# A four-layer image network on one core: five small moves at the seams between its layers

## The chip, the core and the metric

The kernel runs on one core of a Trainium2 chip. A core has five engines with queues of their own: TensorE (PE in the profile; its weight loads are PEld), VectorE (DVE), ScalarE (ACT), GpSimd (POOL) and SyncE (SP), which here only issues transfers. An engine works through its queue in order, and waits on semaphores for what the others have to finish first. The metric is the time of one execution on the device, in microseconds, as the median of the runs shown.

## The reference

Input is a batch of two images of 512 channels x 64 x 64, in fp32. Four layers are applied one after another, each as x = x + layer(groupnorm(x)):

```python
def _gn(v, G=32, eps=1e-5):
    g = v.reshape(B_, G, C_ // G, H_, W_)
    m = mean(g, (2, 3, 4)); s = var(g, (2, 3, 4))
    return ((g - m) / sqrt(s + eps)).reshape(v.shape)

# layer 0: local attention (3x3 window) joined with attention to 16x16 pooled tokens
q = xf @ W_q + b_q;  kv = xf @ W_kv + b_kv
xs = layernorm(mean of gelu(xf @ W_sr + b_sr) over 4x4) ;  kvp = xs @ W_kv + b_kv
attn = softmax(concat([q_scaled . k_local (9), q_scaled . k_pool (256)]))
out = ((lt @ v_local) + (a_pool @ v_pool)) @ W_proj + b_proj

# layer 1: deformable attention: offsets from the query, bilinear samples as keys and values
q = w_q x;  off = tanh(w_off2 gelu(q[::4, ::4] * w_off1 + b_off1)) * 4
kv = w_kv grid_sample(q, grid + off)
out = w_out (softmax(q k / 8) v) + b_out

# layer 2: max pools of 1, 3, ..., 13, mixed by two weights for each channel
s = relu(w2 relu(w1 mean(x) + b1) + b2);  q_s = clip(floor(s), 0, 5)
out = (s - q_s) * pools[q_s + 1] + (q_s + 1 - s) * pools[q_s] + x

# layer 3: linear attention with 256 random features for each of 8 heads
out = (qp @ (kp^T v)) / (qp . sum(kp)) @ Wo
```

All attention has 8 heads of 64 channels.

## The kernel before

An image is held in SBUF as 4 chunks of 128 channels (KC = 4) by 4096 positions; a second buffer of the same size (Y) takes what a layer makes. Positions are worked in 8 blocks of 512 (NB = 8, TB = 512), which is one PSUM bank. The two images are worked one after the other, and in an image the layers one after the other; the seams between layers are interleaved by hand, with Python generators whose `yield` marks where another step may come in. The order of instructions on an engine is the order in which the program writes them, as a tile scheduler rearranges it; a place where the program wants an instruction behind a certain other one is written as `with tc.issue_after(ins)`. For layer 2's last channel chunk VectorE is set to manual schedule, so the order there is as written.

A tile of PSUM or SBUF comes from a pool with a number of buffers. To write into a buffer that comes round again, the writer waits for the last reader of it. Waits are kept for a whole tile, not for parts of it.

**Layer 0** (class Local) goes through 16 units, 4 for each channel chunk, of 1024 positions each. `weigh(u)` (L2677 and following) multiplies the values by nine weights ("taps"), which SyncE fetches from `rows` (L2677), and adds them up on GpSimd (L2706) into `out`, a tile called late in the profile. At its end the unit's result is stored to `yd` in DRAM (L2712), on SyncE's queue. Three of the four passes of the output projection (`output(c4)`, fetches at L2289) read parts of `yd` back; for c4 of 2 and 3 the last chunk is taken from `self.out` in SBUF instead. So units 14 and 15 are never read back from DRAM; unit 13 is, by output(1). Units 13 and 14 are the ones that the change touches.

**Layer 1** starts with `query_and_sample`: a small projection of thinned-out positions fills the four banks of `acc`, from which ScalarE makes off_t (L1255) and VectorE makes bq (L1009, from products of L1006), and then the queries of block 0 are projected (L134, tile wq). Attention follows: `exponentials`, `attended` (psO), `inverse_sums` and `divided`, in a pipeline over blocks and chunks. `inverse_sums` collects the sums of the softmax of the 8 heads in one bank: chunk cc's two heads are rows 32 cc and 32 cc + 1 (L1520), of 32 rows each. VectorE takes the reciprocal of the whole bank in two halves (L1526); `divided` spreads two rows for each chunk over 128 partitions with a product (L1534) and multiplies by it (L1537). `add_output` (L1227, L1230, L1232) projects, adds to the image and takes statistics.

**The seam from layer 1 to layer 2.** For the last block, the statistics of each chunk are joined (L1116), and `pool_mixture` finds from them the mixture weights: L1187 (means of groups), L1188 to L1191, L1194, and on to L1209. Layer 2's horizontal maxima (`across_rows`, L698) are started here, rows by rows, where VectorE has room: rows 0 to 10 and 55 to 64 last (the 128x620 and 128x558 of the profile).

**Layer 2** (`pool_chunk`) goes through the channel chunks. For each it makes larger and larger max pools on VectorE by `spread_max` (L698 for the middle, ScalarE's L699 for edges), and adds the pool of width 2j + 1, times a weight for each channel, into 8 PSUM banks with diagonal weights (L1403), j from 0 to 6. In the last chunk the eighth bank is lent to the statistics of the next group norm until late: the products of block 7 for j < 5 are kept in a list and given out after the fourth product of j = 5. `stats_in_steps` has two steps: means of groups (L965 to L968), and, behind its `yield`, the product L970, nmean on ScalarE (L971), L972 on VectorE and the power on GpSimd (L973). The steps are called at j = 4 and j = 5. At j = 5 the weights of layer 3 are scaled by the result (L1433).

Of the kernel before, what the change touches and what calls it, by code (L numbers as in the profile page):

```python
# [9 lines left out]
F32 = mybir.dt.float32  # L10
# [6 lines left out]
P = 128  # L17
C = 512
KC = C // P
W = 64  # L20
# [913 lines left out]
class Net(General):  # L934
# [22 lines left out]
        for _ in self.stats_in_steps(ks, pp.tile([P, TB], F32, name="mm") if ps is None else ps):  # L957
            pass

    def stats_in_steps(self, ks, ps):  # L960

        nc, mv = self.nc, self.mv
        nmean, rstd, cent, var = (self.stats[:, i, ks] for i in range(4))
        n = ks.stop - ks.start
        nc.tensor.matmul(ps[:, :n], self.grp, mv[:, ks, 0], start=True, stop=True)  # L965
        nc.vector.tensor_tensor(cent, mv[:, ks, 0], ps[:, :n], ALU.subtract)
        nc.vector.tensor_tensor(var, cent, cent, ALU.mult)
        nc.vector.tensor_tensor(var, var, mv[:, ks, 1], ALU.add)  # L968
        yield
        nc.tensor.matmul(ps[:, KC:KC + n], self.grp, var, start=True, stop=True)  # L970
        nc.scalar.mul(nmean, ps[:, :n], -1.0)  # L971
        nc.vector.tensor_scalar(var, ps[:, KC:KC + n], 1e-5, None, ALU.add)  # L972
        nc.gpsimd.tensor_tensor(rstd, var, self.mhalf[:, :n], ALU.pow)  # L973
# [63 lines left out]
    def layer1(self, X, Y, d):  # L1037
# [6 lines left out]
        with tc.tile_pool(name="l1", bufs=1) as sp:  # L1044
# [13 lines left out]
            with tc.tile_pool(name="l1c", bufs=1) as late:  # L1058
# [17 lines left out]
                with tc.tile_pool(name="l1b", bufs=2) as wp, \  # L1076
                        tc.tile_pool(name="l1s", bufs=6, space=PSUM) as pp, \
                        tc.tile_pool(name="l1o", bufs=2, space=PSUM) as ppo:
                    st = wp.tile([P, KC, NB, 6], F32, name="gn_st1", bufs=1)
                    w1 = wp.tile([P, KC, 32], F32, name="w1", bufs=1)  # L1080
                    nc.sync.dma_start(w1, d["w1"].rearrange("(kc p) e -> p kc e", p=P))
                    w2 = wp.tile([32, C], F32, name="w2", bufs=1)
                    nc.sync.dma_start(w2, d["w2"])
                    wo = wp.tile([P, KC, C], F32, name="wo1", bufs=1)
                    nc.sync.dma_start(wo, d["w_out1"].rearrange("(kc p) o -> p kc o", p=P))
                    steps = [(blk, cc) for blk in range(NB) for cc in range(KC)]
                    part = lambda blk, cc=slice(0, KC): Y[:, cc, blk * TB:(blk + 1) * TB]
                    flat = lambda a: a.rearrange("p k o -> p (k o)")
                    probs, totals, later = {}, {}, []
                    rows3 = self.scratch[:, :KC * 10 * W].rearrange("p (k y x) -> p k y x", k=KC, x=W)  # L1090
                    ring = cycle([a[:, n:n + TB] for a, lo, hi in (
                        (flat(wq), 0, KC), (flat(wkv), 5, 8), (flat(feats), 0, 2),
                        (wp.tile([P, 3 * TB], F32, name="totals", bufs=1), 0, 3))
                        for n in range(lo * TB, hi * TB, TB)]).__next__
                    for i in range(len(steps) + 4 + KC):
                        if i < len(steps):
                            blk, cc = steps[i]
                            probs[i], totals[i] = self.exponentials(part(blk, cc), keys[:, cc, :],
                                                                    ring, wp, pp)
                        if 1 <= i <= len(steps):  # L1100
                            blk, cc = steps[i - 1]
                            self.attended(part(blk, cc), probs.pop(i - 1),
                                          vals[:, :, cc * P:(cc + 1) * P], ppo)
                        at = lambda n: i >= n and (i - n) % KC == KC - 1 and (i - n) // KC
                        if (blk := at(1)) is not False and blk < NB:
                            r = self.inverse_sums([totals.pop(KC * blk + n) for n in range(KC)], wp,
                                                  pp)
                        if (blk := at(2)) is not False and blk < NB:
                            self.divided(part(blk), r, pp)
                        if (blk := at(3)) is not False and blk < NB:  # L1110
                            later += [(blk, oc) for oc in range(KC)]
                        if later:
                            blk, oc = later.pop(0)
                            self.add_output(X, wo, part(blk), blk, oc, st, pp)
                            if blk == NB - 1:
                                nc.vector.bn_aggr(self.mv[:, oc, :],  # L1116
                                                  st[:, oc].rearrange("p b s -> p (b s)"))
                                if oc < 2:
                                    self.maxima_across(X, NB - 2, rows3, slice(oc, oc + 1))
                                    self.maxima_down(Y, NB - 2, rows3, slice(oc, oc + 1))  # L1120
                                for rows in ([(20, 32), (32, 44)], [(10, 20), (44, 55)],
                                             [], [])[oc]:
                                    self.across_rows(Y, slice(*rows))
                            elif oc == KC - 1 and blk < NB - 2:
                                self.maxima_across(X, blk, rows3, slice(0, KC))
                                self.maxima_down(Y, blk, rows3, slice(0, KC))
                    mixture = self.pool_mixture(w1, w2, wp, pp)
                    next(mixture)
                    self.maxima_across(X, NB - 1, rows3, slice(0, 1))
                    self.maxima_down(Y, NB - 1, rows3, slice(0, 1))  # L1130
                    for rows in (0, 10), (55, W):
                        self.across_rows(Y, slice(*rows))
                    next(mixture)

    def maxima_across(self, X, blk, h, ks):
# [145 lines left out]
    def query_and_sample(self, X, Y, wq, bq, grid, feats, top, wp, pp, ppk):  # L1281
# [9 lines left out]

        def query(blk):
            for cc in range(KC):
                ps = pp.tile([P, TB], F32, name="mm")
                self.project(ps, wq[:, :, cc * P:(cc + 1) * P], X, blk)
                nc.scalar.activation(Y[:, cc, blk * TB:(blk + 1) * TB], ps, AF.Identity,
                                     bias=bq[:, cc:cc + 1])
                yield
            nc.vector.tensor_reduce(top[:, :, blk], Y[:, :, blk * TB:(blk + 1) * TB], AX.X, ALU.max,
                                    apply_absolute_value=True)  # L1300
# [85 lines left out]
    def pool_chunk(self, X, Y, cc, c0, d0, wts, sp):  # L1386
# [7 lines left out]
            self.pools.insert(0, Y[:, cc - 1, :])  # L1394
        h = image(self.scratch)
        accs, kept = self.accs, []
        stats = self.stats_in_steps(slice(0, KC - 1), accs[NB - 1])
        if cc == KC - 1:
            self.diags = cycle([next(self.diags), next(self.diags),
                                *[sp.tile([P, P], F32, name=f"diag{i}") for i in range(2, 7)]])  # L1400
# [5 lines left out]
        def add(w, src, j):  # L1406
            dg = next(self.diags)
            nc.scalar.activation(dg, self.ident, AF.Copy, scale=w)  # L1408
            for b in range(NB):
                if b == NB - 1 and cc == KC - 1 and j < 5:  # L1410
                    kept.append((b, dg, src, j))
                else:
                    product(b, dg, src, j)
                while kept and j == 5 and b == 3:
                    product(*kept.pop(0))

        add(c0[:, cc:cc + 1], x2, 0)
        flat = Y[:, cc, :]
        for j in range(1, 7):
            if j > 1:  # L1420
                last, flat = image(flat), self.pools.pop(0)
                self.pools.append(flat)
                if cc or j > 2:
                    self.spread_max(h, last, 2)
                self.spread_max(image(flat), h, 1)
                if cc == KC - 1 and j in (4, 5):
                    next(stats, None)
                if cc == KC - 1 and j == 3:
                    self.moments(sp)
                if cc == KC - 1 and j == 5:  # L1430
                    for w in self.wkv3:
                        for kc in range(KC - 1):
                            nc.scalar.activation(w[:, kc], w[:, kc], AF.Copy,  # L1433
                                                 scale=self.stats[:, 1, kc:kc + 1])
            add(wts[:, j, cc:cc + 1], flat, j)
# [78 lines left out]
    def inverse_sums(self, totals, wp, pp):  # L1514
# [6 lines left out]
                                 self.cst[:, C_EVEN + h:C_EVEN + h + 32], totals[cc][h],  # L1521
                                 start=(h == 0), stop=(h == 1))
        r = wp.tile([P, TB], F32, name="recip")
        for i in range(2):
            half = slice(i * TB // 2, (i + 1) * TB // 2)
            nc.vector.reciprocal(r[:, half], psD[:, half])  # L1526
        return r

    def divided(self, att, r, pp):
# [475 lines left out]
class Local:  # L2005
# [673 lines left out]
    def weigh(self, u):  # L2679
# [29 lines left out]
            if i < 9:  # L2709
                yield  # L2710
        lo = u % self.UN * self.UT
        nc.sync.dma_start(self.yd[:, cc, lo:lo + self.UT], out)  # L2712
        yield


# [187 lines left out]
```

## Time and profile before

| | us |
|---|---|
| median of 3 runs | 4915.69 |
| lowest, highest | 4914.85, 4920.11 |
| the profiled execution | 4912.44 |
| its span in the trace | 4910.6 |
| TensorE busy | 4726.7 (96%) |
| VectorE busy | 2983.6 (61%) |
| ScalarE busy | 1851.7 (38%) |
| GpSimd busy | 1815.6 (37%) |

The mean granted clock of TensorE in the profiled execution is 0.989 of full speed. In a row of a timeline the columns are the start and the duration in us, engine, line and operation, what is written and read, and, in square brackets, how long the engine was idle before it and what it waited for. A matmul of fp32 with 512 columns appears as two records in the trace. Most of the product groups follow one another without a gap: TensorE's idle time in the whole span is 4910.6 - 4726.7 = 183.9 us. As an example of a group of SyncE's transfers, there are 32 stores to yd of 512 KB each, and 432 fetches of 256 KB each from rows.

### The profile page before, as it was taken

How to read it: one execution, taken by the hardware profiler on the slowest of the kernel's cores; microseconds unless marked ns; L12 is line 12 of the kernel's file. 1: busy time of each engine (PE TensorE's matmuls, PEld its weight loads, DVE VectorE, ACT ScalarE, POOL GpSimd, SP SyncE). 2: the span in 40 equal slices, each digit the busy share in tenths (PEclk: the TensorE clock that was granted, in tenths of full speed). 3: DMA queues.
4: the chain of work that ended last, by engine and by line, in shares of the span. 5: the costliest groups of instructions: out<-in, count | busy, mean ns of one | idle time of the engine just before them, and what ended most of it. 6: DMA issues, size and time to landing. Idle time of an engine off the chain costs nothing. (4 is left out here: it accounts for less than half of the span.)

```text
span 4910.6 us, 48474 instructions
## 1 busy us (share of the span) xinstructions
PE 4726.7 (96%) x16883; PEld 1965.5 (40%) x16883; DVE 2983.6 (61%) x4044; ACT 1851.7 (38%) x3555; POOL 1815.6 (37%) x1164
## 2 busy tenths in 40 slices
PE   7999999999999999999999999999999999999999
PEld 3433332555334444433344333325543344444333
DVE  4267777754679633377633677777536795334766
ACT  1256665334323233323212566652443233333222
POOL 0036666501320045545400466665013201454544
PEclk9999999999999999999999999999999999999999
DMA  4035556600000000111120455565000000000111
GB/s 157 1 94 156 154 157 169 178 24 10 1 0 19 1 1 1 56 55 56 65 78 2 108 156 157 156 172 160 20 10 1 2 17 1 1 1 18 44 50 46
DMA packets 129441, 313.30 MB, mean 64 GB/s; under 512 B 23394, under 2 KB 36194, under 8 KB 127652
## 3 DMA queue, kind: packets, MB, share of 16 engines
q1 hardware_dynamic: 129188, 310.12, 21.8%
q8 instruction: 135, 2.21, 0.2%
q14 instruction: 118, 0.97, 0.1%
HBM read 260.73 MB, written 49.31 MB: 63 GB/s over the span
## 5 line engine op out<-in xcount | busy, mean ns | idle before, releaser
L134 PE MATMUL mm<-big,w 128*128 128x512 f32 x2496 | 1157.8, 608 | 19.1 <-DVE big L2485 13.6
L134 PEld LDWEIGHTS mm<-big,w 128*128 128x128 f32 x2496 | 453.1, 191 | 689.7 <-issue 549.0
L2706 POOL TENSOR_TENSOR late<-late,big 128x1024 f32<-128x1024 f32 x194 | 459.2, 2367 | 216.6 <-DVE big L2701 174.4
L1702 POOL TENSOR_TENSOR big<-big 128x512 f32<-128x512 f32 x224 | 277.6, 1271 | 219.3 <-ACT big L1693 219.3
L2526 DVE TENSOR_TENSOR prods<-qs,big 128x2048 f32<-128x2048 f32 (+1 forms) x184 | 330.7, 1819 | 34.3 <-PE tap L2564 23.7
L2701 DVE TENSOR_TENSOR big<-big,mm 128x512 f32<-128x512 f32 x388 | 252.4, 682 | 104.6 <-ACT mm L2693 103.2
L1693 ACT ACTIVATE big<-mm,ed 128x256 f32<-128x256 f32 x512 | 194.1, 490 | 232.7 <-DVE top L1689 200.3
L2693 ACT COPY mm<-big 128x512 f32<-128x512 f32 x432 | 245.4, 597 | 80.3 <-DMA big<-rows 46.1
L2706 POOL TENSOR_TENSOR late<-late,tap 128x1024 f32<-128x1024 f32 x94 | 222.0, 2361 | 97.8 <-DVE tap L2701 83.7
L1501 POOL TENSOR_TENSOR wq<-prob 128x512 f32<-128x512 f32 x48 | 71.9, 1520 | 486.3 <-ACT prob L1498 474.8
L1689 DVE TENSOR_REDUCE top<-mm 128x1 f32<-128x512 f32 x256 | 159.0, 683 | 148.2 <-PE mm L1620 148.2
L2611 POOL TENSOR_TENSOR late<-late 128x512 f32<-128x512 f32 x76 | 95.4, 1275 | 395.7 <-ACT late L2596 379.5
L134 PE MATMUL mm<-big,wq 128*128 128x512 f32 x512 | 235.0, 604 | 2.7 <-ACT off_t L1255 2.7
L1227 PE MATMUL mm<-big,wo 128*128 128x512 f32 x512 | 237.6, 610 | 0.0
L1667 PE MATMUL mm<-w,big 128*128 128x512 f32 x512 | 234.5, 601 | 0.0
L1403 PE MATMUL acc<-big,diag 128*128 128x512 f32 x512 | 227.7, 602 | 5.2 <-ACT diag L1408 4.6
L1961 PE MATMUL mm<-k,w 128*128 128x512 f32 x512 | 232.0, 600 | 0.7 <-DVE big L1964 0.7
L973 POOL TENSOR_TENSOR group_stats<-group_stats,cst 128x1 f32<-128x1 f32 (+1 forms) x20 | 20.2, 1024 | 543.0 <-DVE group_stats L972 489.7
L134 PE MATMUL mm<-big,big 128*128 128x512 f32 x464 | 201.7, 594 | 0.5 <-DVE b_sr L1011 0.5
L1926 POOL TENSOR_SCALAR qf_sum<-qf,ksum_ratio 128x512 f32<-128x512 f32 x64 | 100.4, 1570 | 264.2 <-PE psD L1944 212.4
L1498 ACT ACTIVATE prob<-mm 128x512 f32<-128x512 f32 x256 | 133.3, 602 | 171.3 <-PE mm L1495 171.1
L2564 PE MATMUL tap<-prods,cst 128*32 128x512 f32 x1152 | 183.2, 604 | 11.5 <-DVE prods L2526 7.4
(432 smaller groups left out, 8118.7 us busy)
## 6 DMA issues: line engine op xcount, KB each, us to landing
big<-rows SPq DMA_DIRECT2D x432, 256.0 KB
tap<-rows SPq DMA_DIRECT2D x208, 256.0 KB
yd<-late SPq DMA_DIRECT2D x32, 512.0 KB
lost_all<-lost SPq DMA_DIRECT2D x128, 128.0 KB
out<-big SPq DMA_DIRECT2D x64, 256.0 KB
big<-in_W_kv SPq DMA_DIRECT2D x8, 1024.0 KB
rows<-late SPq DMA_DIRECT2D x64, 128.0 KB
big<-in_x SPq DMA_DIRECT2D x32, 256.0 KB
```

The source lines that it names most:

```text
L134: self.nc.tensor.matmul(ps, w[:, kc, :], X[:, kc, blk * TB:(blk + 1) * TB], start=(kc == 0), stop=(kc == KC - 1))
L1227: nc.tensor.matmul(ps, w[:, kc, oc * P:(oc + 1) * P], att[:, kc, :], start=(kc == 0), stop=(kc == KC - 1))
L1403: nc.tensor.matmul(accs[b], dg, src[:, b * TB:(b + 1) * TB], start=(j == 0), stop=(j == 6))
L1667: nc.tensor.matmul(ps, X[:, kc, lo:lo + P], wv[:, kc, :], start=(kc == 0), stop=(kc == KC - 1))
L1693: nc.scalar.activation(f[:, t, :], pS[h][i][:, t % 2, :], AF.Exp, bias=ed[:, t, 2 * cc + h:2 * cc + h + 1])
L1702: nc.gpsimd.tensor_tensor(a, a, part, ALU.add)
L1961: nc.tensor.matmul(ps, self.wo[:, kc, oc * P:(oc + 1) * P], qs[:, kc, :], start=(kc == 0), stop=(kc == KC - 1))
L2526: self.nc.vector.tensor_tensor(self.pair(u, k)[:, :n].rearrange("p k (y x) -> p k y x", x=W), bcast(qs.rearrange("p (y x) -> p y x", x=W), ...
L2564: nc.tensor.matmul(ps[32 * q:32 * q + 32, :], self.cst[:, C_TAPW + 16 - 2 * k:][:, :32], self.pair(u, k)[:, 0, j * TB:(j + 1) * TB], start ...
L2693: nc.scalar.copy(ps, part)
L2701: nc.vector.tensor_tensor(part.rearrange("p (y x) -> p y x", x=W), self.vx[:, y:y + self.UY // 2, dx:dx + W], ps.rearrange("p (y x) -> p y ...
L2706: nc.gpsimd.tensor_tensor(out, out, t, ALU.add)
```

## The change

Five places are edited.

- A: `inverse_sums` transposes the bank in 32x32 squares, so that the two rows of each 32 that carry sums become two columns, takes the reciprocal of those columns alone (128x32), and transposes back.
- B: the maxima of rows 0 to 10 and 55 to 64 are issued behind the last chunk's aggregate (L1116), where before they could come ahead of it.
- C: in layer 2's last chunk, `stats_in_steps` gets one more `yield`, between L970 and L971; both of its first steps are called at j = 4, and the last one between the two maxima of j = 5. The kept products are given out ahead of j = 5's products, not after its fourth.
- D: the first query of layer 1 takes the last bank of `acc` in place of a bank of the pool.
- E: the stores of units 13 and 14 go on GpSimd's queue.

```diff
-    def stats_in_steps(self, ks, ps):
+    def stats_in_steps(self, ks, ps, split=False):
...
         nc.tensor.matmul(ps[:, KC:KC + n], self.grp, var, start=True, stop=True)
+        if split:
+            yield
         nc.scalar.mul(nmean, ps[:, :n], -1.0)
         nc.vector.tensor_scalar(var, ps[:, KC:KC + n], 1e-5, None, ALU.add)
         nc.gpsimd.tensor_tensor(rstd, var, self.mhalf[:, :n], ALU.pow)
...
                             if blk == NB - 1:
-                                nc.vector.bn_aggr(self.mv[:, oc, :],
-                                                  st[:, oc].rearrange("p b s -> p (b s)"))
+                                mean = nc.vector.bn_aggr(
+                                    self.mv[:, oc, :], st[:, oc].rearrange("p b s -> p (b s)"))
...
-                    for rows in (0, 10), (55, W):
-                        self.across_rows(Y, slice(*rows))
+                    with tc.issue_after(mean.ins):
+                        for rows in (0, 10), (55, W):
+                            self.across_rows(Y, slice(*rows))
                     next(mixture)
...
-                ps = pp.tile([P, TB], F32, name="mm")
+                ps = acc[:, KC - 1] if not blk + cc else pp.tile([P, TB], F32, name="mm")
                 self.project(ps, wq[:, :, cc * P:(cc + 1) * P], X, blk)
...
-        stats = self.stats_in_steps(slice(0, KC - 1), accs[NB - 1])
+        stats = self.stats_in_steps(slice(0, KC - 1), accs[NB - 1], True)
...
             nc.scalar.activation(dg, self.ident, AF.Copy, scale=w)
+            while kept and j == 5:
+                product(*kept.pop(0))
             for b in range(NB):
                 if b == NB - 1 and cc == KC - 1 and j < 5:
                     kept.append((b, dg, src, j))
                 else:
                     product(b, dg, src, j)
-                while kept and j == 5 and b == 3:
-                    product(*kept.pop(0))
...
                     self.spread_max(h, last, 2)
+                if cc == KC - 1 and j == 5:
+                    next(stats, None)
                 self.spread_max(image(flat), h, 1)
-                if cc == KC - 1 and j in (4, 5):
-                    next(stats, None)
+                if cc == KC - 1 and j == 4:
+                    next(stats)
+                    next(stats)
...
         r = wp.tile([P, TB], F32, name="recip")
-        for i in range(2):
-            half = slice(i * TB // 2, (i + 1) * TB // 2)
-            nc.vector.reciprocal(r[:, half], psD[:, half])
+        nc.vector.transpose(psD, psD)
+        two = psD.rearrange("p (b n r) -> p b n r", n=16, r=2)[:, :, 0]
+        nc.vector.reciprocal(two, two)
+        nc.vector.transpose(r.rearrange("p (b n r) -> p b n r", n=16, r=2), bcast(two, 2, 16))
         return r
...
         lo = u % self.UN * self.UT
-        nc.sync.dma_start(self.yd[:, cc, lo:lo + self.UT], out)
+        queue = nc.gpsimd if 2 <= KC * self.UN - u <= 3 else nc.sync
+        queue.dma_start(self.yd[:, cc, lo:lo + self.UT], out)
         yield
```

## The prediction

> **What bounds the kernel now.** I read the page first, then the waits of TensorE, then the timeline around each wait that the change touches.
>
> ```profile
> PE 4726.7 (96%) x16883; PEld 1965.5 (40%) x16883; DVE 2983.6 (61%) x4044; ACT 1851.7 (38%) x3555; POOL 1815.6 (37%) x1164
> ```
>
> TensorE (PE) is busy for 4726.7 of 4910.6 us, so it bounds the kernel. All its gaps together are 183.9 us. No part of the change takes work off TensorE: only its gaps, and stretches in which its clock is lowered, can move the time. The waits of PE (instruction, what released it, us in total, times, longest) name four that the change touches:
>
> ```profile
> PE mm L1187 <- DVE channels_mv L1116: 5.7, 2, 2.8
> PE acc L1403 <- DVE group_stats L972: 5.4, 2, 2.7
> ...
> PE mm L1534 <- DVE recip L1526: 4.2, 2, 2.1
> ...
> PE mm L134 <- ACT off_t L1255: 2.7, 2, 1.3
> ```
>
> "2 times" is once for each image. These four are 18.0 us, the most that can be won from waits, 0.37% of the time. A measurement of this kernel tells about 0.2% (9.8 us) from no change.
>
> **Part A, the inverse sums.** Two reciprocals of 128x256 are removed; a transpose, a reciprocal of 128x32 and a transpose are put in their place. Layer 0 already does the same three operations at the same shapes, so the prices are in the groups:
>
> ```profile
> L1526 DVE RECIPROCAL recip<-mm 128x256 f32<-128x256 f32 x32 | 53.9, 1726 | 88.5 <-PE mm L1520 88.5
> L2646 DVE STREAM_TRANSPOSE mm<-mm 128x512 f32<-128x512 f32 x32 | 23.4, 731 | 25.7 <-PE mm L2621 25.7
> L2649 DVE STREAM_TRANSPOSE late<-mm 128x512 f32<-128x512 f32 x32 | 22.9, 717 | 1.1
> L2648 DVE RECIPROCAL mm<-mm 128x32 f32<-128x32 f32 x32 | 11.7, 366 | 1.0
> ```
>
> Old: 3.36 us for the pair at the seam. New: 731 + 366 + 717 ns, about 1.8 to 1.9 us. VectorE saves 1.5 us in each of 16 blocks, but TensorE waits for L1526 only in the last block of an image; in the other 14 VectorE has slack, and the saving is worth nothing. Gain: 1.5 us in each image, 3.0 us. The end follows, since L1534, L1537 and 40 records of L1227 come one after the other.
>
> Behind this wait lies a second cost, which only one image pays:
>
> ```profile
> 1449.16 1.59 PE L1534 MATMUL mm<-recip,cst 2*128 2x512 f32 x8 [2.13 <-DVE recip L1526]
> 1450.69 20.33 PE L1227 MATMUL mm<-big,wo 128*128 128x512 f32 x40
> ...
> 3887.29 1.14 PE L1534 MATMUL mm<-recip,cst 2*128 2x512 f32 x8 [2.11 <-DVE recip L1526]
> 3888.36 17.43 PE L1227 MATMUL mm<-big,wo 128*128 128x512 f32 x40
> ```
>
> The same work takes 1.59 + 20.33 us in image 1 and 1.14 + 17.43 in image 2. The window from 1450 to 1453 has a granted clock of 0.50, that from 3888 to 3891 of 1.00. So a lowered clock behind this gap cost 2.90 + 0.45 = 3.35 us, in image 1 alone. [...] I follow the row: with a gap of 0.6 us left, the 3.35 us go too. [...]
>
> **Part B, maxima behind the last mean.** Two maxima (L698, 0.80 and 0.73 us on VectorE) move from before the last aggregate (L1116) to behind it. L1187, which waits 2.84 us for L1116, starts about 0.85 us earlier: one of the two had lain in the chain, the other in VectorE's own wait for TensorE. Behind it the scheduler sets the first between L1116 and L1189, where VectorE waited 0.89 us for ScalarE anyway. The second comes between L1189 and L1190, on the path to L1194, and delays it by 0.65 us. Net 0.2 us in an image, 0.4 in all; bounds: 0 (both on the path again) and 1.7 (both hidden).
>
> **Part C, layer 2's seam.** With 3968 elements a row each, L698's maxima take VectorE 4.29 us, four to a map in j=5. TensorE stands before j=5:
>
> ```profile
> 1658.42 4.29 DVE L698 TENSOR_TENSOR pool<-wkv 128x3968 f32<-128x3968 f32 x1
> 1662.86 3.67 PE L1403 MATMUL acc<-pool,diag 128*128 128x512 f32 x8 [2.69 <-DVE group_stats L972]
> 1662.86 4.89 POOL L973 TENSOR_TENSOR group_stats<-group_stats,cst 128x3 f32<-128x3 f32 x1 [185.68 <-DVE group_stats L972]
> 1667.14 4.29 DVE L698 TENSOR_TENSOR big<-wkv 128x3968 f32<-128x3968 f32 x1
> 1667.78 3.79 ACT L1433 ACTIVATE w<-w,group_stats 128x512 f32<-128x512 f32 x6 [4.56 <-POOL group_stats L973]
> 1674.09 6.17 PE L1403 MATMUL acc<-big,diag 128*128 128x512 f32 x14
> ```
>
> The releaser named is L972, but it is queued behind the L698 that ends at 1662.71; j=5's map is what PE really waits for. The kept products (5, each 2 records of 0.43 us, so 4.3 us) ran after that. Now they run before j=5 and fill the gap, if L972, which frees their bank, comes early: it is moved between j=5's two maxima, at 1658.4, in time. j=5 then ends at about 1671.2 instead of 1674.09.
>
> What is late next is j=6's map, by the last L698 (1667.14 to 1671.43 before). Its edge columns come from ScalarE (L699, 1662.80 before), and ScalarE takes its queue in order: the six scalings L1433 now stand ahead of L699. They wait for the power on GpSimd (L973). That took 4.89 us beside L698, where the shape takes about 0.55 alone. So it starts at 1658.6, ends at about 1663.5, the scalings (3.79) at 1667.3, L699 (0.42) at 1667.7, the last maximum at 1672.0, and j=6 begins at 1672.05. Gain 2.0 us an image, 4.0 in all; about 0.9 us of waiting is left. Bounds: 2.7 (no delay), and -2.4 if the power is held by a second maximum too (rival 2).
>
> **Part D, the first query's bank.** The first query no longer waits for a bank that off_t (L1255) frees:
>
> ```profile
> 1018.76 5.37 PE L134 MATMUL mm<-big,wq 128*128 128x512 f32 x8 [1.34 <-ACT off_t L1255]
> 3458.59 3.67 PE L134 MATMUL mm<-big,wq 128*128 128x512 f32 x8 [1.34 <-ACT off_t L1255]
> ```
>
> It takes the last bank of acc, whose last reader is VectorE's copy L1009 (1017.53, 0.16 us), so PE starts at about 1017.8: 0.95 us earlier, 1.9 in both images (bounds 0 and 2.7). The next chunk needs a bank at about 1021.3; off_t ends at 1019.98, so no new wait. Here too image 1 alone pays a half clock behind the gap: 5.37 - 3.67 = 1.70 us, gone if the gap of 0.4 us no longer lowers the clock.
>
> **Part E, two stores on GpSimd's queue.** The stores of units 13 and 14 leave SyncE's queue, where each held the fetches behind it until GpSimd's last sum:
>
> ```profile
> 898.28 0.33 SPq L2712 DMA_DIRECT2D yd<-late  x1
> ```
>
> For unit 14 (945.00) the tap fetches of unit 15 start about 2.5 us earlier, and output(3)'s third fetch moves ahead of them. But from 955.35 to 974 VectorE works without a pause in an unchanged order and PE waits for it, not for taps: I take 0 (bounds 0 and 2.5 an image: what the fetches gain).
>
> The store itself has no row: the trace before has no transfer on GpSimd's queue. Issue on SyncE takes 0.33 us. GpSimd idles 2.64 us behind the first store and 9.9 behind the second, so an issue of that size is covered. Landing is read by two: output(1) fetches unit 13 back (at 902.3), and ScalarE's L2604 of unit 15 overwrites the same buffer at 904.94 (image 1) and 3344.06 (image 2), 6.7 and 4.9 us after GpSimd's sum. [...] I take 0.
>
> **Sum.** Waits: 3.0 + 0.4 + 4.0 + 1.9 + 0 = 9.3 us. Clock: 3.35 + 1.70 = 5.05. Together 14.4: the profiled execution goes from 4912.44 to 4898.0. The median of the runs, 4915.69, stands 3.25 us above the profiled one, about one lowered stretch. From it: 4901.3.
>
> **The rivals.**
> 1. Waits go, clock does not: the lowered stretches fall behind other gaps. For it: they come and go between the two images. Against it: fewer gaps are left. 4915.69 - 9.3 = 4906.4.
> 2. Part C's scalings are late. GpSimd's power is held through a second L698 (4.3 us): scalings until 1671.6, L699 1672, the last maximum 1676.4, j=6 at 1676.5, 2.4 us later than before. For it: the 4.89 us above are a block by one L698. Against it: there the next L698 began at 1667.14 and the power still ended by 1667.75. 8.8 us worse than forecast: 4910.1.
> 3. Slower: unit 13's store lands late. L2604, SyncE's fetches behind the read of yd and unit 15's chain all stand on it. At a landing 14 us after the release, ScalarE is held 14 - 6.7 = 7.3 us in image 1 and 9.1 in image 2, and with a half clock (3.4 us lost) behind each gap that is 23.2 us against 9.3 of waits won: +14, about 4930. On the same count it decides from a landing of 7 us (nothing left of the gain), and is slower by over 0.2% from 12. For it: the DMA engines are at 90% there, shared with the fetches. Against it: the store only changes queues.
> 4. The change isn't in the order: the same instructions are counted on PE and ACT, VectorE has 16 more and GpSimd 4 transfers more; the order of both kernels shows every move. Left out.
>
> **How the numbers follow.** As worked out 0.54 (own range 4896 to 4906); rival 1 0.22; rival 2 0.11; rival 3, with stores late by other means, 0.13. Faster by over 0.2% means below 4905.9: nearly all of the first and a little under half of rival 1, 0.62. Within 0.2%: the rest of rival 1, rival 2 and the edge of the first, 0.25. Slower: 0.13. The range runs from 4893 (part B or C at its upper bound) to 4911 (rival 2).
>
> **What would show it.** Right: L1534's wait at 0.6, L1187's at 2.0, L1403's behind L970 gone with 0.9 before j=6, L134's first query at 0.4, and no half clock behind L1534 or that query. Wrong: a wait of PE on L2604 or on yd's fetch near 905 and 3345; L973 over 5 us with PE waiting more than 3 us before j=6; or a clock of 0.50 in as many windows as before.

## The result, and the profile after

The changed kernel takes 4900.05 us (median of 22 runs, 4895.45 to 4904.91). The kernel before, in 22 runs beside it, takes 4912.52 (4902.65 to 4920.11); with more runs its median lies 3.2 us lower than the one that the prediction started from. The ratio is 0.9977, 95% interval 0.9971 to 0.9983: 11.3 us faster, 8.4 to 14.2 (the difference of the two medians, 12.5, lies inside). The profiled execution went from 4912.44 to 4903.24 us, its span from 4910.6 to 4901.4.

The page's engine line of the changed kernel:

```profile
PE 4725.6 (96%) x16883; PEld 1967.4 (40%) x16883; DVE 2958.7 (60%) x4060; ACT 1850.1 (38%) x3555; POOL 1817.1 (37%) x1168
```

TensorE's work is the same, 4725.6 us against 4726.7. Its gaps went from 183.9 to 175.8 us. VectorE has 24.9 us less, part A's saving over 16 blocks, of which the end sees only two. The waits of TensorE after, at the places of the change (line numbers are now a few higher):

```profile
PE mm L1190 <- DVE channels_mv L1118: 4.0, 2, 2.0
...
PE mm L1197 <- DVE pool_var L1194: 2.8, 2, 1.4
...
PE mm L1541 <- DVE recip L1533: 1.2, 2, 0.6
...
PE acc L1406 <- DVE big L698: 1.0, 2, 0.5
...
PE acc L134 <- DVE bq L1011: 0.8, 2, 0.4
```

The timeline of TensorE after, at A's seam of both images and at D's of image 1:

```profile
1445.46 1.14 PE L1541 MATMUL mm<-recip,cst 2*128 2x512 f32 x8 [0.63 <-DVE recip L1533]
1446.53 17.43 PE L1230 MATMUL mm<-big,wo 128*128 128x512 f32 x40
...
3878.99 1.14 PE L1541 MATMUL mm<-recip,cst 2*128 2x512 f32 x8 [0.62 <-DVE recip L1533]
3880.06 17.43 PE L1230 MATMUL mm<-big,wo 128*128 128x512 f32 x40
```

```profile
1016.77 3.67 PE L134 MATMUL acc<-big,wq 128*128 128x512 f32 x8 [0.41 <-DVE bq L1011]
```

The gaps are what was worked out (0.6 and 0.4 us), and image 1 now takes 17.43 and 3.67 us, what image 2 took before for the same work, at a granted clock of 1.00 (1445.46 to 1464 and 1016.77 to 1020.44). At layer 2's seam, all engines:

```profile
1650.83 4.29 DVE L698 TENSOR_TENSOR pool<-wkv 128x3968 f32<-128x3968 f32 x1
1650.95 4.89 POOL L975 TENSOR_TENSOR group_stats<-group_stats,cst 128x3 f32<-128x3 f32 x1 [181.25 <-DVE group_stats L974]
1655.23 4.29 DVE L698 TENSOR_TENSOR wkv<-pool 128x3968 f32<-128x3968 f32 x1
1655.87 3.79 ACT L1439 ACTIVATE w<-w,group_stats 128x512 f32<-128x512 f32 x6 [4.68 <-POOL group_stats L975]
1656.89 7.03 PE L1406 MATMUL acc<-pool,diag 128*128 128x512 f32 x16
1659.56 0.40 ACT L699 COPY wkv<-pool 128x128 f32<-128x128 f32 x1
1660.00 4.29 DVE L698 TENSOR_TENSOR big<-wkv 128x3968 f32<-128x3968 f32 x1 [0.48 <-ACT wkv L699]
1664.44 5.82 PE L1406 MATMUL acc<-big,diag 128*128 128x512 f32 x13 [0.52 <-DVE big L698]
```

Here the path is seen as it was described: GpSimd's power takes 4.89 us beside one maximum and is done at 1655.84, 0.6 us after the next maximum has begun; the six scalings stand ahead of the edge copy L699, and the last maximum waits 0.48 us for that copy. The wait before j = 5 is gone; 0.52 us is left before j = 6. And the store of unit 13:

```profile
897.94 0.79 POOL L2720 DMA_DIRECT2D yd<-late  x1 [0.31 <-POOL late L2713]
900.27 2.50 POOL L2618 TENSOR_TENSOR late<-late 128x512 f32<-128x512 f32 x2 [1.54 <-ACT late L2603]
903.24 0.58 ACT L2611 COPY late<-mm 128x512 f32<-128x512 f32 x1 [1.57 <-DMA yd<-late]
```

It does hold ScalarE's copy of unit 15, by 1.57 us (1.50 in image 2). Nothing of that reaches TensorE.

In gaps at its own places the change won, for both images together: A 2 x 1.50, B 2 x 0.33, C 2 x 2.17, D 2 x 0.93, that is 9.9 us. All gaps together fell by 8.1, since other waits came out 1.8 us longer in this execution; 0.8 of that are two waits for fetches of yd that the trace of before doesn't have. In that profile the clock won next to nothing: the stretches at 0.50 sum to 105.6 us before and 103.9 after.

### The profile page after: what moved, and what is told of

Its sections match the earlier page's. It is cut to its first block, busy times and chain, and to the rows that moved or that the text cites. A ratio compares the mean times of both kernels' runs of the same rounds, so it can differ in the third digit from the quotient of the medians.

```text
span 4901.4 us, 48498 instructions
## 1 busy us (share of the span) xinstructions
PE 4725.6 (96%) x16883; PEld 1967.4 (40%) x16883; DVE 2958.7 (60%) x4060; ACT 1850.1 (38%) x3555; POOL 1817.1 (37%) x1168
```

## The experiments

Ratios are to the kernel before, run on the same chip beside each.

**A and D alone**, the two parts with a lowered clock behind their gap in the trace of before:

```diff
+                ps = acc[:, KC - 1] if not blk + cc else pp.tile([P, TB], F32, name="mm")
...
+        nc.vector.transpose(psD, psD)
+        two = psD.rearrange("p (b n r) -> p b n r", n=16, r=2)[:, :, 0]
+        nc.vector.reciprocal(two, two)
+        nc.vector.transpose(r.rearrange("p (b n r) -> p b n r", n=16, r=2), bcast(two, 2, 16))
```

> The kernel before with parts A and D alone. All theories: TensorE's wait before L1530-L1538's spreading product falls from 2.1 to 0.6 us, that before the first query from 1.34 to 0.41, together 4.9 us in both images. Theory 1 (the prediction: the lowered clock behind these two gaps goes with them): ratio to before about 0.9980 (-10 us), and no granted clock of 0.5 within 10 us behind either place. Rival (a lowered stretch that is not met here is met at the next gaps): ratio about 0.9990 (-4.9 us), as many windows at 0.5 as before. Both: all other waits as before (2.8 us before L1187's twin, 2.7 us before j=5).

Measured: 0.9981 (0.9973 to 0.9989), -9.3 us, with gaps of 0.62 and 0.41 us and no half clock behind them. That is nearly twice the 4.9 us of waits, and the waits alone lie just outside the interval (5.4 to 13.3 us). Theory 1 holds for these two places. What other gaps make of the clock is the subject of the tables below.

**B and C alone**, and the same kernel again (the main lines of the edit):

```diff
+        if split:
+            yield
...
+            while kept and j == 5:
+                product(*kept.pop(0))
...
+                    with tc.issue_after(mean.ins):
```

> The kernel before with parts B and C alone. Theory 1 (sum of waits): TensorE waits 1.98 us for the last aggregate (2.84 before) and 1.38 before the second product of the mixture (0.85 before), 0 before j=5 (2.69 before) and 0.5 before j=6; 0.33 + 2.2 us an image, ratio about 0.9990 (-5.0 us). Rival (parts depend on each other): if A or D had made room for C, the wait before j=5 stays over 1 us here. The waits of 2.1 us behind the sums and 1.34 us before the first query stay.

> Parts B and C alone once more, since their first timing gave a ratio of 1.0 (0.9992 to 1.0008) where 5.0 us of waits were gone. Theory 1 (the waits count in full; the first figure was scatter, from the lowered clock and from waits for fetches of yd, which were 3.0 us in that profile): ratio 0.9985 to 0.9992. Rival (something that the profile's waits do not show takes the 5 us back): 0.9996 to 1.0004 again.

Measured: 1.0000 (0.9992 to 1.0008) and 0.9999 (0.9990 to 1.0007), in 13 runs each. Yet the waits fell as expected; the waits of TensorE in the second of these profiles:

```profile
PE mm L1190 <- DVE channels_mv L1118: 4.0, 2, 2.0
...
PE mm L1197 <- DVE pool_var L1194: 2.7, 2, 1.4
...
PE acc L1406 <- DVE big L698: 1.0, 2, 0.5
```

So 5.0 us of gaps went, and no time with them: the rival of the second expectation holds. The first profile had 3.0 us of waits for fetches of yd, the second had none, so those are not the reason. What the timed runs list beside each time is the mean granted clock; the last table below is made from it.

**B alone** and **C alone**:

> The kernel before with part B alone. B and C together had timed as 1.0 twice where 5 us of waits were gone. Theory 1 (waits count in full): 0.7 us in all, ratio 0.9995 to 1.0003, not told from no change. Rival (B costs what C wins): 1.0006 or more.

> The kernel before with part C alone. Theory 1 (waits count in full): TensorE's waits before j = 5 and j = 6 fall from 5.4 to about 1.0 us in sum, ratio about 0.9991 (-4.3 us). Rival (C's gain is taken back by stretches of lowered clock further on, which the earlier seam meets at another phase of the gate): 0.9996 to 1.0004.

Measured: B 1.0004 (0.9995 to 1.0013), C 0.9994 (0.9985 to 1.0003). Neither run decides: the interval of B holds both of its theories (1.0003 and 1.0006), and that of C holds -4.3 us and zero.

**Part E alone, and all but part E:**

```diff
-        nc.sync.dma_start(self.yd[:, cc, lo:lo + self.UT], out)
+        queue = nc.gpsimd if 2 <= KC * self.UN - u <= 3 else nc.sync
+        queue.dma_start(self.yd[:, cc, lo:lo + self.UT], out)
```

> The kernel before with part E alone. Theory 1 (no effect: VectorE sets the end of layer 0): ratio 1.000, TensorE's waits of 1.5, 0.7 and 1.8 us near 957, 961 and 970 unchanged. Theory 2 (earlier fetches help): up to -5 us, 0.999, and those three waits shorter. Theory 3 (the store lands late): ScalarE's copy of unit 15 waits 1 to 2 us for the store on GpSimd's queue (0 in before), TensorE waits about 0.4 us for a fetch of yd in one or both images, +0 to +1 us.

> The changed kernel with its two stores back on SyncE's queue (parts A to D alone). Theory 1: as the changed kernel within 1 us, ratio to before 0.9977 to 0.9980; the sum of TensorE's waits is lower by about 0.8 us if the two waits of 0.4 us for fetches of yd come from part E, and the same if they do not. Rival (part E earns part of the gain): ratio 0.9985 or above.

Measured: E alone 0.9996 (0.9988 to 1.0004); without E 0.9971 (0.9960 to 0.9982). E neither wins nor costs anything that can be measured. TensorE in the profile of E alone, where the earlier fetches might have helped:

```profile
953.57 1.25 PE L2295 MATMUL qs<-sq,late 128*128 128x512 f32 x2 [1.51 <-DVE big L2300]
957.27 3.83 PE L2295 MATMUL qs<-sq,big 128*128 128x512 f32 x8 [0.74 <-DVE big L2300]
966.64 3.83 PE L2295 MATMUL mm<-sq,big 128*128 128x512 f32 x8 [1.83 <-DVE big L2701]
```

The three waits are unchanged to 0.01 us (1.51, 0.73 and 1.83 before). ScalarE's copy of unit 15 waited 2.3 us for the store, in one image, as theory 3 has it, and the time doesn't show it. The short waits of TensorE for fetches of yd (twice 0.4 us in the changed kernel) appear without E too, 1.4 us in that profile, and in the profile of A and D alone: they come and go with the transfers, and E has no part in them.

**The statistics late**, to see what lets C's kept products fill the wait:

```diff
-                if cc == KC - 1 and j == 5:
-                    next(stats, None)
                 self.spread_max(image(flat), h, 1)
+                if cc == KC - 1 and j == 5:
+                    next(stats, None)
```

> The changed kernel with the last step of the statistics (L973 to L975) back behind both maxima of j = 5; the kept products stay ahead of j = 5. Theory 1 (the kept products can fill the wait only because L974 frees their bank early): the wait before the products stays near 2.7 us, named L974, and the kept products run behind it, so TensorE is 2.2 us later an image than in the changed kernel. Rival (the kept products alone fill the wait): no wait over 0.6 us there.

Measured in its profile:

```profile
1656.41 1.10 PE L1406 MATMUL acc<-pool,diag 128*128 128x512 f32 x2 [2.59 <-DVE group_stats L974]
```

The whole wait is back, 2.6 us in each image, and the kept products run behind it. (There is one run of this kernel, 4905.34 us; the reading is from its trace.) Of C's two moves, the early L974 is the one that makes the other possible.

**All stores on GpSimd's queue.** This was meant to show from where a late store costs:

```diff
-        queue = nc.gpsimd if 2 <= KC * self.UN - u <= 3 else nc.sync
+        queue = nc.gpsimd if u < KC * self.UN - 1 else nc.sync
```

> The changed kernel with the stores of units 0 to 14 on GpSimd's queue (only unit 15's stays on SyncE's): 30 such stores in place of 4. Theory 1 (a store lands 5 to 8 us after its issue, and GpSimd and the readers have room for that): ratio to before as the changed kernel's, 0.9971 to 0.9983. Rival (late stores cost: each holds ScalarE's copy into the same buffer, two units on, and GpSimd spends 0.6 to 0.8 us on each issue): ScalarE waits for yd in more than ten units, TensorE's wait grows by 0.5 to 1 us a unit, ratio over 1.000.

Measured: 0.9955 (0.9940 to 0.9970), median 4890.23 us. Neither theory had that: it is 10 us faster than the changed kernel. ScalarE waited for a store of yd only once, 1.1 us, not in more than ten units. The reason stands in a wait that neither the change nor the prediction had looked at, the third largest of TensorE (the two above it are one wait for the first weights, 24.9 us, and 26 waits of at most 0.5). Before, and with all stores moved:

```profile
PE mm L2602 <- DVE late L2698: 12.9, 4, 5.2
```

```profile
PE mm L2609 <- DVE late L2705: 3.5, 2, 1.8
```

The timeline of the changed kernel near 846 us tells how it comes about:

```profile
843.86 2.37 POOL L2713 TENSOR_TENSOR late<-late,big 128x1024 f32<-128x1024 f32 x1
846.25 0.33 SPq L2720 DMA_DIRECT2D yd<-late  x1
846.75 1.12 SPq L2684 DMA_DIRECT2D big<-rows  x2
851.90 1.11 ACT L2700 COPY mm<-big 128x512 f32<-128x512 f32 x2 [8.47 <-DMA big<-rows]
852.52 1.28 DVE L2705 TENSOR_TENSOR late<-late,mm 128x512 f32<-128x512 f32 x2 [5.51 <-ACT mm L2700]
853.86 3.95 PE L2609 MATMUL mm<-late,vp 128*64 128x512 f32 x8 [4.69 <-DVE late L2705]
```

The store of unit 12 stands in SyncE's queue until GpSimd's last sum; the fetches behind it start at 846.75, and ScalarE, VectorE and TensorE wait for them one after another, TensorE 4.69 us. It is the mechanism of part E, one unit earlier than part E applies it.

**Unit 12's store alone:**

```diff
-        queue = nc.gpsimd if 2 <= KC * self.UN - u <= 3 else nc.sync
+        queue = nc.gpsimd if KC * self.UN - u == 4 else nc.sync
```

> The changed kernel with one store moved, another than the change's: unit 12's goes on GpSimd's queue, those of 13 and 14 back on SyncE's. Theory 1 (unit 12's store is the one that held the fetches on which TensorE waited near 854 and 3288 us): the waits named L2705 fall from 12.5 to about 3.5 us in sum, as with all stores moved, ratio to before about 0.9955. Rival (it took the earlier stores of units 0 to 11 too): 0.9965 to 0.998, with a wait over 3 us left there.

Measured: 0.9953 (0.9939 to 0.9966), median 4886.27 us. Its wait, and its timeline:

```profile
PE mm L2609 <- DVE late L2705: 3.1, 2, 1.5
```

```profile
838.84 1.11 SPq L2684 DMA_DIRECT2D big<-rows  x2
...
845.02 0.79 POOL L2720 DMA_DIRECT2D yd<-late  x1 [0.31 <-POOL late L2713]
845.24 1.11 ACT L2700 COPY mm<-big 128x512 f32<-128x512 f32 x2 [3.32 <-DMA big<-rows]
```

The fetches go out at 838.84, 6 us ahead of the store, and the waits named L2705 are 3.1 us in sum. With the wait goes the lowered clock behind it: in each of the eleven profiles with unit 12's store on SyncE's queue TensorE waits 4.5 to 5.3 us there, in both images, and a stretch at 0.50 begins in the last 3 us of that wait; in the three with the store on GpSimd's queue there is neither. One store of 16 gives all that moving 15 of them gives.

**Two more moves for what is left of B and C.** First without E, with the maxima of rows 55 to 64 behind pool_var and the six scalings written between j = 6's maxima:

```diff
-                    with tc.issue_after(mean.ins):
-                        for rows in (0, 10), (55, W):
-                            self.across_rows(Y, slice(*rows))
+                    for rows, ins in ((0, 10), mean), ((55, W), self.pool_var):
+                        with tc.issue_after(ins.ins):
+                            self.across_rows(Y, slice(*rows))
...
```

> Parts A to D without E, and two more moves: the maxima of rows 55 to 64 go behind pool_var (L1194) instead of between L1192 and L1193, and the scalings of layer 3's weights (L1439) go between the two edge copies of j = 6 instead of ahead of them. Theory 1 (what stands in the chain is what the traces name): the wait before L1197 falls from 1.38 to 0.85 us and that before j = 6 from 0.52 to 0, 2.1 us in all, ratio to before about 0.9970. Rival (GpSimd's power L1199 or the first use of the scaled weights is now late): a wait over 1.6 us before L1203, or over 1 us before L987.

Measured: 0.9970 (0.9958 to 0.9981). The wait before L1197 fell to 0.85 us. That before j = 6 stayed at 0.52: the scheduler had left the scalings ahead of the edge copy, so this half of the edit moved nothing. Then with all stores moved, and the scalings held behind the edge copy explicitly:

```diff
+                if cc == KC - 1 and j == 6:
+                    with self.tc.issue_after(edge.ins):
+                        for w in self.wkv3:
+                            for kc in range(KC - 1):
+                                nc.scalar.activation(w[:, kc], w[:, kc], AF.Copy,
+                                                     scale=self.stats[:, 1, kc:kc + 1])
...
```

> All stores but unit 15's on GpSimd's queue, the maxima of rows 55 to 64 behind pool_var, and the six scalings of layer 3's weights held behind the first edge copy of j = 6 with issue_after (in the run before, the scheduler had left them ahead of it). Theory 1 (each wait named by the trace is paid in full): the wait before L1197 is 0.85 us, that before j = 6 at most 0.1, so 2.1 us less than with all stores moved, ratio to before about 0.9950. Rival (the scalings are now late for layer 3's first products): a wait over 1 us before L988.

Measured: 0.9950 (0.9937 to 0.9964), median 4886.98 us. The wait before j = 6 is gone from the list, those before layer 3's first products are as before (0.8 us at most), and the scalings wait for the power only 0.23 us, behind the edge copy:

```profile
1648.79 0.43 ACT L699 COPY wkv<-pool 128x128 f32<-128x128 f32 x1 [4.03 <-DVE pool L698]
...
1649.44 3.79 ACT L1434 ACTIVATE w<-w,group_stats 128x512 f32<-128x512 f32 x6 [0.23 <-POOL group_stats L975]
```

Its 2.1 us cannot be told apart in time from unit 12's store alone. By their ratios both beat the changed kernel by 12 to 13 us.

**The clock, from all fourteen profiles** (thirteen kernels, one of them twice). In each of them the stretches at 0.50 begin on a grid of 3.413 us that runs through the whole execution, with another offset in each, and last one to four cells of it. I cut each execution on its grid, from 27 us on, and asked how often a cell in which TensorE stood idle for so long was followed by a cell at half clock. Cells that were themselves at half clock are counted apart:

```
                        cell at full clock       cell at half clock
TensorE idle, us        cells   half next        cells   half next
0    to 0.25            17607        0             214        7
0.25 to 1.0              1474       17              67       48
1.0  to 1.5               265       69              17       17
1.5  to 1.75               85       12               8        8
1.75 to 2.0                29       22              21       21
2.0  and more             118      117              63       63
```

So what counts is the idle time of a cell, and about half a cell is enough: from 1.75 us on it is 139 of 147. It is added over the gaps of a cell: 20 of these cells have no single gap over 1.7 us, and half clock followed all 20. Between 0.25 and 1.75 us the idle time alone doesn't decide, and what else does stays open. A stretch that has begun goes on with less: 48 of 67 cells at half clock with 0.25 to 1.0 us idle were followed by another, against 17 of 1474 at full clock. The windows view of before at D's seam shows both outcomes for one gap; columns are the cell, its length, the busy time of PE, PEld, DVE, ACT and POOL, the granted clock, the DMA share and GB/s:

```profile
1016.23:1019.64 3.41, 1.93 (x10) 1.46 (x11) 0.45 (x2) 2.96 (x6) 0.00 (x0) 1.00 0.15 56
1019.64:1023.05 3.41, 3.41 (x5) 1.35 (x4) 0.00 (x0) 0.35 (x1) 0.00 (x0) 0.50 0.02 5
```

```profile
3456.76:3460.17 3.41, 2.07 (x9) 1.28 (x9) 0.45 (x2) 2.62 (x5) 0.00 (x0) 1.00 0.02 5
3460.17:3463.59 3.42, 3.42 (x14) 1.58 (x13) 0.00 (x0) 0.92 (x2) 0.00 (x0) 1.00 0.00 0
```

In image 1 the cell took in the gap of 1.34 us and a piece of the one ahead of it, in image 2 the gap alone. Over the six profiles that still have the long gaps, the gap of 1.34 us was followed by half clock 10 times of 12: 6 of 6 where its cell had 1.38 to 1.50 us idle, 3 of 5 where it had the gap alone, and once out of a cell that was at half clock already. That of 2.1 us was followed by it 10 times of 12, each time with the whole gap in one cell. In the two other cases a line of the grid cut the gap in two, as in image 2 of before (1.66 and 0.45 us):

```profile
3883.42:3886.83 3.41, 1.76 (x5) 0.45 (x3) 3.41 (x3) 0.00 (x0) 0.00 (x0) 1.00 0.00 0
3886.83:3890.25 3.42, 2.96 (x13) 1.25 (x14) 3.39 (x7) 0.00 (x0) 0.00 (x0) 1.00 0.02 5
```

Over the eight that have the short gaps it was 1 of 16 (0.41 us) and 0 of 16 (0.63 us).

Last, the mean granted clock over all timed runs of a kernel, as time lost, which is the time of a run multiplied by (1 - clock). The clock is listed to 0.001 in each run, which is 4.9 us, so only means over many runs can be read. Before loses 52.0 us in the mean of 77 runs, 52.5, 53.0 and 50.3 on the three chips; each row is set against the runs of before beside it (the change, whose neighbours have no clock on record, against all 77), with one standard error. "Gaps" is what the named waits lost, and "sum" adds it to the change of lost time:

```
kernel                    runs  lost, us  against before  gaps, us    sum   mean time against before
A and D                     13    49.4     -3.0 +- 1.3      -4.9      -7.9     -8.2
B and C, both runs          26    55.9     +3.3 +- 1.2      -5.0      -1.7     -0.8
B                           11    52.3     +2.0 +- 2.3      -0.7      +1.3     +0.4
C                           11    51.8     +1.5 +- 2.3      -4.3      -2.8     -1.5
E                           14    50.2     -2.3 +- 1.7       0        -2.3     -1.4
A to D                       7    49.7     -2.7 +- 1.6      -9.9     -12.6    -12.1
the change                  22    49.9     -2.1 +- 1.1      -9.9     -12.0    -12.1
two more moves, no E         7    46.9     -6.1 +- 2.3     -11.0     -17.1    -16.0
all stores moved             4    45.2     -7.8 +- 1.9     -19.3     -27.1    -24.1
unit 12's store              5    41.1     -9.2 +- 2.9     -19.7     -28.9    -23.4
all stores, two moves        5    43.0     -7.3 +- 1.7     -21.0     -28.3    -24.9
```

The two columns at the right agree within 1.3 us in the first eight rows. In the three with unit 12's store moved the sum goes 3.0 to 5.5 us too far. A part of that is that "lost" also counts half-clock time in which TensorE stood idle: in the trace of before it was busy for 81.1 of the 105.6 us at 0.50, and behind unit 12's wait in the changed kernel the stretch begins at 851.70, TensorE at 853.86. Within one execution the account closes: TensorE's busy time, less half of what it was busy at half clock, is 4685 to 4688 us in all fourteen profiles. So executions differ by their gaps and by that half.

So B and C together were not timed wrongly: their gaps went, and about 3 us more were lost at lowered clock. B alone and C alone read 2.0 and 1.5 us more, neither clear of its scatter, so it stays open whether each part brings its share or only the two together do. Why they meet more of the lowered clock was not tried; that the total hangs on where all later gaps fall on the grid is likely, and not shown.

## Why the prediction was right or wrong, point by point

- **A, D:** 1.5 and 0.95 us an image were forecast, 1.50 and 0.93 measured. The rows of layer 0's transposes and reciprocal gave the price at once; the three measured 730, 366 and 716 ns.
- **B:** 0.2 us an image forecast, 0.33 measured: 0.86 less before the aggregate's product, 0.53 more before the next one, where 0.65 was taken. The run with the second maximum moved on took those 0.53 back.
- **C:** 2.0 forecast, 2.17 measured; the path (bank, scalings, edge copy, last maximum) came out step by step. Rival 2 fell: the power ended 0.7 us after the first maximum, not after a second. (The 0.55 us taken for it alone is that of the form 128x1; 128x3 has no row without a maximum beside it.)
- **E:** nothing forecast, nothing measured. No run showed beforehand how long such a store takes to land, so the 0 taken for it was the author's estimate. In the changed kernel an issue on GpSimd takes 0.59 to 0.79 us, where the 0.33 of SyncE stood in the prediction, and the store landed after 5.1 to 7.9 us (median 6.5). The DMA engines are 94 to 97% busy in the 6.5 us behind each of the four issues; that this is what made it late was not tried. It passed the slack of 4.9 us, and rival 3's wait did appear, 1.5 us on ScalarE in each image. But TensorE doesn't show it, nor does the time of E alone, so the rival's break-even of 7 us was set too low.
- **The clock:** the term that failed in size. 5.05 us were forecast, from image 1's loss in one execution. At the two seams that was rather too little: long gaps were followed by half clock 20 times of 24, 12 of 12 in image 1 and 8 of 12 in image 2, which was put at nothing, and the short ones once in 32 (that gaps of 0.6 and 0.4 us would leave the clock up was the author's estimate). But the mean loss over the execution fell only from 52.0 to 49.9 us, 2.1 us. In the profile after, stretches begin behind other gaps, at 967.75, 1186.20, 1694.79 and 2111.22, where before has none. So a sign of being wrong that the prediction named did appear: about as many windows at 0.50 as before. Another appeared too, a wait for a fetch of yd near 3345 (0.41 us at 3342.39), though the kernel without E has such waits as well.
- **The number** came out better than its terms, and that is in part luck. The waits gave 9.9 us for 9.3, the clock 2.1 for 5.05. The result, -11.3 us, lies between rival 1 (-9.3) and the likeliest case (-14.4). That the median is near the forecast 4901.3 is also because the starting median was 3.2 us high.
- **What the prediction missed:** it looked at the waits that the change touches, and read part E as two stores. The list that it was made from names L2602 with 12.9 us, more than any of the four. Behind 9.8 of these stood the store one unit ahead of part E's.

## What to carry to other kernels

Order the waits of the bounding engine by size before judging which ones an edit removes, and follow each back through the queues to what is issued late; here one store in a queue of fetches was worth as much as five edits at the seams. A gap cost its length here, and, where the idle time of a cell of 3.413 us added up to 1.75 us or more (139 cells of 147), half of TensorE's busy time in each cell that then ran at half clock (with that half taken off, the busy time is 4685 to 4688 us in all fourteen profiles). The first stands in each execution; the second changes from one to the next, so it is to be read as a mean over many runs, not from one.

## What the runs showed of the hardware that was not expected

- The granted clock changed on a grid of 3.413 us that was fixed within an execution, in all fourteen profiles. At full clock, idle time of 2.0 us or more in a cell was followed by half clock 117 times of 118, under 0.25 us never in 17607. The same gap of 2.1 us was followed by it 10 times of 10 inside one cell, and not once of 2 when the grid cut it.
- At half clock less idle time kept the clock low: 0.25 to 1.0 us did so in 48 cells of 67, against 17 of 1474 at full clock.
- A store of 512 KB on GpSimd's queue landed after 5.1 to 7.9 us in the changed kernel (four stores), while the DMA engines, 94 to 97% busy, were shared with fetches. It took GpSimd 0.59 to 0.79 us to issue there, and 0.57 us near 846 us with all stores moved.
- Two edits that together removed 5.0 us of waits left the time as it was, in two sets of 13 runs, and 3.3 us (+- 1.2) more were lost at lowered clock.
